# A two-layer graph kernel: fewer warm-up matmuls, list steps spread wider, paired tiles in the half chunk, and row stores later in the sync queue

## The chip, the cores and the metric

The kernel runs on one core of one Trainium2 chip. The metric is the device time of one execution in microseconds (us); lower is better. The five engines of the core have queues of their own: TensorE (PE, its weight loads shown as PEld), VectorE (DVE), ScalarE (ACT), GpSimd (POOL) and SyncE (SP), which here only issues transfers. Transfers are carried by the core's 16 DMA engines.

## The reference, cut to what matters

The data are 3327 nodes with 512 features and a weighted adjacency matrix of 3327 x 3327 that is dense in its first rows and columns ("hubs") and sparse elsewhere.

```python
# layer 0
h = jnp.maximum(_layernorm(x), 0.0)
u = jax.nn.relu(adj @ (h @ W1) + b1)          # W1: 512 x 128
x = x + adj @ (u @ W2) ... + b2               # computed as (adj @ u) @ W2 + b2
# layer 1
h = jnp.maximum(_layernorm(x), 0.0)
type_sum = adj @ h
attn_a, attn_b = sigmoid([type_sum, h] @ Wa.T + ba), sigmoid([type_sum, h] @ Wb.T + bb)
s_left, s_right = h @ W_sa @ a_sa[0, :512], h @ W_sa @ a_sa[0, 512:]
e = where(adj != 0, exp(-leaky_relu(s_left[:, None] + s_right[None, :], 0.01)), 0)
x_a = (e / (e.sum(1) + 1e-5)) @ (h @ W_sa)
x_b = adj @ (h @ W_gcnb) + b_gcnb
x = x + sigmoid(attn_a * x_a + attn_b * x_b)
```

The products with `adj` are the cost. Layer 0 has two of them, and the kernel makes each as a dense pass over the whole matrix. For layer 1 it gathers, for each group of 32 nodes, only the rows of h and the columns of adj in which something stands; which ones these are, it finds out during the first dense pass.

## The kernel before

The arrays are padded to 26 blocks of 128 rows (3328). The transposed matrix is read in column chunks: six of 512 columns and one of 256, the half chunk. There are three stages: the first dense pass (`acc_u`, 7 chunks of 26 blocks), the second dense pass (`acc_g`, 7 chunks), and the gather stage of layer 1.

The head warms TensorE up while the first rows of x are loaded and normalized:

```python
WAKE = 30
...
awake = bank(psB, "awake")
for _ in range(WAKE):
    nc.tensor.matmul(awake[:, :P], ident, ident, start=True, stop=True)
```

A tile of the matrix; both passes share eight buffers of 128 x 512 values, and all these loads are in the sync queue:

```python
def load_adj(j, c, name, n=1):
    c0, w = chunks[c]
    n = min(n, NB - j)
    t = adjp.tile([P, CW], F32, tag="adj", name=f"{name}_{c}_{j}")
    t = t[:, : n * w].rearrange("p (k i) -> p k i", i=w)
    rows = adjT[j * P : (j + n) * P, c0 : c0 + w]
    nc.sync.dma_start(t, rows.rearrange("(k p) i -> p k i", p=P))
    return t
```

The first pass. In its first chunk the rows are also normalized (`normalize`), transposed (`turn_h`, tile `pt`) and multiplied with W1 (`make_u`, tile `pu`). VectorE reduces every tile to the largest absolute value per group of 32 columns (`most`), from which the lists are made:

```python
for c in range(NCH):
    c0, w = chunks[c]
    acc = bank(psA, f"acc_u_{c}")
    most = l0w.tile([P, MG, NB], F32, tag="most", name=f"most_{c}")
    for j in range(NB):
        if c == 0:
            ...                       # load_x(j + 4), normalize(j + 3), turn_h(j + 2), make_u(j + 1)
        with queued(x_loaded[min(j + 4, NB - 1)] if c == 0 else None):
            a = load_adj(j, c, "a1")[:, 0, :]
        added = nc.tensor.matmul(acc[:, :w], u[j], a[:, :w], start=(j == 0), stop=(j == NB - 1))
        with queued(...):
            nc.vector.tensor_reduce(most[:, : w // GW, j], a[:, :w].rearrange(...), ...)
        if j >= 2:
            next(lists, None)         # one step of the lists of the chunk before
        if j % 3:
            gather_behind(added)      # GpSimd: one gather of columns, paced by this matmul
        ...
    chunk_end = make_g(c, acc)        # ScalarE: gT <- acc_u; PE: four transposes pg; VectorE: g
    with tc.issue_after(chunk_end.ins):
        if c == 1:
            load_weights()            # W2, b2 (then b2_row + 0.5 on VectorE), W_sa, ...
        ...
    lists = make_lists(c, most)
    next(lists)
```

The lists are made by a generator, a step at each `next`; what stands between two `yield` is put beside one block of the pass:

```python
def make_lists(c, most):
    ...                               # VectorE: flag, upto (a scan), count, after
    nc.vector.tensor_tensor(after[:, :n, :], ..., upto[:, :n, :], ALU.subtract)
    p_off = bank(psB, f"p_off_{c}")
    nc.tensor.matmul(p_off[:, :n], before, count[:, :n], start=True, stop=True)
    nc.tensor.matmul(p_off[:, MG : MG + n], every, count[:, :n], start=True, stop=True)
    ...                               # VectorE: offset, size
    nc.tensor.matmul(p_sh[:, : n * NB], shift, after[:, :n, :].rearrange(flat), ...)
    ...                               # VectorE: step
    yield
    ...
    for batch in batches:             # one to three batches for a chunk
        for i, q in batch:
            for h in range(2):
                nc.vector.tensor_scalar(at[:, k : k + r, h, :], place_row..., offset..., op0=ALU.is_ge)
            if (i, q) != batch[-1]:
                yield
        pl = bank(psB, f"p_list_{f0}")
        for i, q in batch:
            ...                       # PE: 2 * rooms[i] small matmuls p_list <- step, at
        yield
        ...                           # VectorE: past, jb, row_h, row_a
        listed.update(batch)
        yield
```

The second pass loads tiles for `per = CW // w` blocks, so the half chunk is paired there already. Beside each chunk stands the row work of the chunk before (`late`, one step at every second block):

```python
def make_h1(c, sT):
    c0, w = chunks[c]
    blocks = range(c0 // P, (c0 + w) // P)
    for b, i in enumerate(blocks):
        x1 = xs.pop(i)
        with tc.high_priority():
            ...                       # PE: px; VectorE: x1 = px + x1; ScalarE's queue: store of x1
            h = hrow[i % NR]
            _, last_row[0] = ln_relu(h[:, :D], x1, l0w, f"b{i}")
            score(i, h[:, :D], 1, h[:, D : D + 1])
            nc.sync.dma_start(h_dram[i * P : (i + 1) * P, :], h)
        if c:
            rows_made.add(i)
        yield
    for i in blocks:
        last_row[1] = score(i, hrow[i % NR][:, :D], 0, node[i][:, 0:1])
        yield
    ...                               # PE: four transposes pl <- node; ScalarE: s_left
    rows_made.update(blocks)
    yield
    for i in blocks:
        if c < NCH - 2:
            own_logits(i, ...)
        yield
```

`h_dram` is the table of h rows from which the gather stage later takes its rows. `acc_hub` matmuls for the first 128 nodes are mixed into the second pass from its third chunk on.

Of the kernel before, what the change touches and what calls it, by code (L numbers as in the profile page):

```python
# [26 lines left out]
SEG = 4  # L27
WAKE = 30
LN_EPS = 1e-5
# [17 lines left out]
def kernel(  # L47
# [35 lines left out]
    def bank(pool, name):  # L83
        return pool.tile([P, CW], F32, tag="bank", name=name)
# [94 lines left out]
    def queued(*insts):  # L179

        behind = ExitStack()
        for inst in insts:
            if inst is not None:
                behind.enter_context(tc.issue_after(inst.ins))
        return behind
# [30 lines left out]
    with (  # L216
# [167 lines left out]
        def make_lists(c, most):  # L384
# [5 lines left out]
            def small(shape, name, dtype, bufs=2):  # L390
# [16 lines left out]
                upto[:, :n, :], ALU.subtract,  # L407
            )
            p_off = bank(psB, f"p_off_{c}")
            nc.tensor.matmul(p_off[:, :n], before, count[:, :n], start=True, stop=True)  # L410
# [24 lines left out]
            for batch in batches:  # L435
# [7 lines left out]
                for i, q in batch:  # L443
                    r, k = rooms[i], col[i, q]
                    for h in range(2):
# [5 lines left out]
                        )  # L451
                    if (i, q) != batch[-1]:
                        yield
                pl = bank(psB, f"p_list_{f0}")
# [40 lines left out]
        for c in range(NCH):  # L495
            c0, w = chunks[c]
            acc = bank(psA, f"acc_u_{c}")
            most = l0w.tile([P, MG, NB], F32, tag="most", name=f"most_{c}")
            for j in range(NB):
                if c == 0:  # L500
# [6 lines left out]
                    if j + 1 < NB:  # L507
                        make_u(j + 1)
                with queued(x_loaded[min(j + 4, NB - 1)] if c == 0 else None):
                    a = load_adj(j, c, "a1")[:, 0, :]  # L510
                added = nc.tensor.matmul(  # L511
# [51 lines left out]
        def own_logits(i, junk):  # L563
# [6 lines left out]
            nc.vector.tensor_tensor(node[i][:, 1:3], node[i][:, 1:3], bab_row, ALU.add)  # L570

        def make_h1(c, sT):

            c0, w = chunks[c]
# [4 lines that stand above are left out]
# [8 lines left out]
                    score(i, h[:, :D], 1, h[:, D : D + 1])  # L587
                    nc.sync.dma_start(h_dram[i * P : (i + 1) * P, :], h)
                if c:
                    rows_made.add(i)  # L590
                yield
            for i in blocks:
                last_row[1] = score(i, hrow[i % NR][:, :D], 0, node[i][:, 0:1])
                yield
            pl = bank(psB, f"pl_{c}")
# [10 lines left out]
            if c == 0:  # L606
                nc.scalar.copy(s_hub, pl[:, :P])
            rows_made.update(blocks)
            yield
            for i in blocks:  # L610

                if c < NCH - 2:
                    own_logits(i, l0w.tile([P, D], BF16, tag="junk", name=f"junk_{i}", bufs=1))
                yield
# [482 lines left out]
```

## Time and profile before

| | |
|---|---|
| time, median of 3 runs | 781.73 us (780.81 to 782.48) |
| span of the profiled execution | 780.7 us, 12235 instructions |
| PE, PEld | 755.4 us (97%), 415.5 us (53%) |
| VectorE, ScalarE, GpSimd | 517.5 us (66%), 185.5 us (24%), 489.8 us (63%) |
| DMA | 200.15 MB, mean 256 GB/s |
| loads of 128 x 512 tiles, sync queue | 325 of 256 KB, median 4.0 us from issue to landing |
| loads of 128 x 256 tiles, sync queue | 26 of 128 KB, median 3.3 us |
| stores of h rows, sync queue | 26 of 260 KB, median 4.1 us |
| first dense pass, second dense pass | to 225.07 us, from there to 431.60 us |

In the profile one line is a group of instructions: line of the kernel, engine, operation, output and inputs, shape, count; a time in brackets is how long the engine stood idle before it and what ended that. A 128x512 matmul on 32-bit values stands as two records. The ends of matmuls are modelled, so where one waits for its data it may look busy; the distance between the starts of two records tells more. The issue of a transfer is not counted as busy.

### The profile page before, as it was taken

What the parts mean: (1) busy time and instruction counts of PE and PEld (TensorE: products, weight loads), DVE (VectorE), ACT (ScalarE), POOL (GpSimd) and SP (SyncE); (2) the same over time, 40 slices, a digit from 0 to 9 for tenths busy, and PEclk for the clock granted to TensorE, in tenths of its full rate; (3) what the DMA queues carried; (4) which work ended last, traced back from release to release, by engine and by line L of the source; (5) the groups of instructions that cost most, each with busy time, mean ns of one, the idle gap of its engine ahead of it and who ended that gap; (6) DMA issues with size and microseconds to landing.
All of it is one profiled execution on the core that took longest, in us unless ns stands there. A gap on an engine that the chain in (4) does not pass through costs nothing.

```text
span 780.7 us, 12235 instructions
## 1 busy us (share of the span) xinstructions
PE 755.4 (97%) x3647; PEld 415.5 (53%) x3647; DVE 517.5 (66%) x1658; ACT 185.5 (24%) x396; POOL 489.8 (63%) x513
## 2 busy tenths in 40 slices
PE   9999989999999999999999999999999999999995
PEld 8775434444544344344446456665665666655453
DVE  6768979999992876759577575555465464644542
ACT  6882000000000331403215212221221221311211
POOL 1400746666777777777773277677777777777720
PEclk9999999999999999999999999999999999999998
DMA  7888899889889999899998578688888888888840
GB/s 241 247 261 262 272 296 289 263 270 293 230 262 288 319 333 336 283 323 318 311 336 266 171 226 242 202 245 255 252 238 253 251 234 260 225 258 229 228 154 32
DMA packets 107099, 200.15 MB, mean 256 GB/s; under 512 B 17009, under 2 KB 30864, under 8 KB 107024
## 3 DMA queue, kind: packets, MB, share of 16 engines
q1 hardware_dynamic: 72800, 124.40, 48.7%
q0 software_dynamic: 25536, 63.74, 29.8%
q10 hardware_dynamic: 8688, 11.15, 4.3%
q8 instruction: 31, 0.51, 0.3%
q14 instruction: 44, 0.36, 0.2%
HBM read 179.39 MB, written 20.55 MB: 256 GB/s over the span
## 4 chain that ended last, share of the span: by engine, by line
PE 82%; DMA 7%; DVE 7%; issue 1%; ACT 1%; POOL 0%; SPq 0%; POOLq 0%; ACTq 0%; DVEq 0%
PE acc_u L511 16%; PE acc_g L665 14%; PE acc L809 13%; PE p_b L863 12%; PE p_a L870 11%; DMA a<-in_adjT_dram 6%; PE ptt L823 3%; PE pu L293 3%; PE acc_hub L624 2%; PE px L580 2%; PE p_list L459 2%; PE pt L285 1%; DVE junk L559 1%; DVE xb L583 1%; PE awake L100 1%
## 5 line engine op out<-in xcount | busy, mean ns | idle before, releaser
L139 POOL DMA_INDIRECT ae<-in_adjT_dram,row_a x228 | 244.2, 1071 | 145.2 <-DVE most L515 49.1
L139 POOL DMA_INDIRECT hr<-h_rows,row_h x140 | 143.5, 1025 | 47.0 <-issue 27.4
L511 PE MATMUL acc_u<-a,rows 128*128 128x512 f32 (+1 forms) x364 | 164.0, 580 | 1.5 <-DMA a<-in_adjT_dram 1.5
L665 PE MATMUL acc_g<-a,g 128*128 128x512 f32 (+1 forms) x364 | 156.4, 570 | 3.6 <-DMA a<-in_adjT_dram 3.4
L139 POOL DMA_INDIRECT rows<-h_rows,row_h x88 | 90.0, 1022 | 50.7 <-DVE e_hub L206 24.2
L515 DVE TENSOR_REDUCE most<-a 128x16 f32<-128x512 f32 (+1 forms) x182 | 111.1, 640 | 7.2 <-DMA a<-in_adjT_dram 6.8
L665 PEld LDWEIGHTS acc_g<-a,g 128*128 128x128 f32 x364 | 68.2, 192 | 80.1 <-issue 62.7
L863 PE MATMUL p_b<-W_g_sb,tyT 128*128 128x257 f32 x416 | 97.1, 386 | 0.8 <-ACT tyT L836 0.5
L870 PE MATMUL p_a<-W_sa_sb,tyT 128*128 128x512 f32 (+2 forms) x216 | 93.5, 577 | 0.0
L863 PEld LDWEIGHTS p_b<-W_g_sb,tyT 128*128 128x128 f32 x416 | 76.6, 189 | 30.8 <-DVE ae L206 7.3
L511 PEld LDWEIGHTS acc_u<-a,rows 128*128 128x128 f32 x364 | 63.9, 192 | 52.3 <-issue 45.8
L838 DVE COPY tyT<-ptt 128x512 f32<-128x512 f32 x51 | 34.9, 686 | 73.6 <-PE ptt L823 73.5
L809 PE MATMUL acc<-hr,ae 64*64 64x512 f32 x560 | 68.0, 607 | 0.0
L870 PEld LDWEIGHTS p_a<-W_sa_sb,tyT 128*128 128x128 f32 x216 | 41.0, 190 | 37.7 <-issue 35.9
L728 ACT ACTIVATE f<-f 128x2 f32<-128x2 f32 x26 | 5.3, 203 | 173.2 <-DVE f L727 145.8
L809 PE MATMUL acc<-rows,ae 64*64 64x512 f32 x352 | 42.5, 594 | 2.5 <-issue 1.8
L809 PEld LDWEIGHTS acc<-hr,ae 64*64 64x64 f32 x560 | 29.8, 136 | 23.4 <-issue 22.9
L302 ACT ACTIVATE gT<-acc_u,b_col 128x512 f32<-128x512 f32 (+1 forms) x7 | 4.6, 656 | 154.8 <-PE acc_u L511 97.9
L696 DVE TENSOR_TENSOR xb<-xb,b_row 128x512 f32<-128x512 f32 x26 | 17.7, 690 | 29.7 <-DMA xb<-in_x_dram 24.1
L559 DVE SCALAR_TENSOR_TENSOR junk<-rows,w_rows 128x512 bf16<-128x512 f32 x52 | 35.7, 687 | 1.9 <-ACT rows L201 0.9
L583 DVE TENSOR_TENSOR xb<-px,xb 128x512 f32<-128x512 f32 x26 | 16.9, 683 | 24.9 <-PE px L580 24.9
L823 PEld LDWEIGHTS ptt<-ident,ty 128*128 128x128 f32 x208 | 24.2, 141 | 14.2 <-issue 12.9
(142 smaller groups left out, 909.9 us busy)
## 6 DMA issues: line engine op xcount, KB each, us to landing
a<-in_adjT_dram SPq DMA_DIRECT2D x325, 256.0 KB, 4.0
h_rows<-rows SPq DMA_DIRECT2D x26, 260.0 KB, 4.1
x<-in_x_dram SPq DMA_DIRECT2D x26, 256.0 KB, 3.4
xb<-in_x_dram SPq DMA_DIRECT2D x26, 256.0 KB, 5.0
x<-xb ACTq DMA_DIRECT2D x26, 256.0 KB, 2.1
x1b<-x SPq DMA_DIRECT2D x26, 256.0 KB, 4.9
out_dram<-va SPq DMA_DIRECT2D x25, 256.0 KB
ae<-in_adjT_dram,row_a POOLq DMA_INDIRECT x228, 4.4
```

Source lines behind the costliest of these rows:

```text
L139: return nc.gpsimd.indirect_dma_start(out=dst, out_offset=None, in_=table, in_offset=bass.IndirectOffsetOnAxis(ap=rows, axis=0), bounds_ch ...
L293: nc.tensor.matmul(pu[:, :HID], hT[:, k, :], W1_sb[:, k, :], start=(k == 0), stop=(k == KD - 1))
L511: added = nc.tensor.matmul(acc[:, :w], u[j], a[:, :w], start=(j == 0), stop=(j == NB - 1))
L515: nc.vector.tensor_reduce(most[:, : w // GW, j], a[:, :w].rearrange("p (b i) -> p b i", i=GW), axis=AX.X, op=ALU.max, apply_absolute_value ...
L559: return nc.vector.scalar_tensor_tensor(junk, h, 1.0, w_rows[:, s, :], op0=ALU.mult, op1=ALU.mult, accum_out=into)
L583: nc.vector.tensor_tensor(x1, px, x1, ALU.add)
L665: added = nc.tensor.matmul(acc[:, :w], g[j], a[:, j % per, :], start=(j == 0), stop=(j == NB - 1))
L809: added = nc.tensor.matmul(taken[i]["acc"][h][q * HALF : (q + 1) * HALF, :], both[half_p, q * n + k, :], taken[i][k0][k][half_p, q, :D], s ...
L823: moved = nc.tensor.transpose(pt[:, k * P : (k + 1) * P], ty[h][:, k * P : (k + 1) * P], ident)
L838: last = nc.vector.tensor_copy(dst, src)
L863: nc.tensor.matmul(p_b[n][:, :WH], tyT[:, k, 0, :], W_g_sb[:, k, n * WH : (n + 1) * WH], start=(k == 0), stop=(k == KD - 1),)
L870: last = nc.tensor.matmul(p_a[:, c0:c1], tyT[:, k, 1, :], W_sa_sb[:, k, c0:c1], start=(k == 0), stop=(k == KD - 1),)
```

## The change

There are four edits; the first three concern the first pass, the last one the second.

- The head has 18 warm-up matmuls instead of 30.
- The list generator yields twice as often at its ends: once after `after`, before the p_off matmuls, and after every item of a batch, the last too. So the matmuls of a list step come a step later than the VectorE work that they read.
- In the half chunk of the first pass one load brings the tiles of two blocks, as in the second pass.
- The store of a row block in the h table is no longer issued where the row is made, but by a later step of the row work: block by block, from the third `score` step on. In the program that is ten to twelve blocks later. In the sync queue the four stood together behind the load of block 12 (of the next chunk); now they stand one by one behind the loads of blocks 13, 15, 17 and 19. The last two chunks' stores keep their places in the queue.

The aim is to have TensorE start earlier on real work, to keep it from waiting for VectorE's list work and for small tiles, and to keep tile loads from standing in the sync queue behind stores whose rows aren't made yet.

```diff
-WAKE = 30
+WAKE = 18
@@ make_lists
                 upto[:, :n, :], ALU.subtract,
             )
+            yield
             p_off = bank(psB, f"p_off_{c}")
@@ make_lists, batches
-                    if (i, q) != batch[-1]:
-                        yield
+                    yield
                 pl = bank(psB, f"p_list_{f0}")
@@ first pass
             acc = bank(psA, f"acc_u_{c}")
+            per = CW // w
@@
-                with queued(x_loaded[min(j + 4, NB - 1)] if c == 0 else None):
-                    a = load_adj(j, c, "a1")[:, 0, :]
+                if j % per == 0:
+                    with queued(x_loaded[min(j + 4, NB - 1)] if c == 0 else None):
+                        tile_a = load_adj(j, c, "a1", per)
+                a = tile_a[:, j % per, :]
@@ make_h1
+        def store_row(i):
+            nc.sync.dma_start(h_dram[i * P : (i + 1) * P, :], hrow[i % NR])
+
@@
-                    nc.sync.dma_start(h_dram[i * P : (i + 1) * P, :], h)
+                    if c == NCH - 1:
+                        store_row(i)
                 if c:
                     rows_made.add(i)
                 yield
-            for i in blocks:
+
+            unstored = iter(blocks if c < NCH - 1 else ())
+
+            def store_next():
+                for i in unstored:
+                    store_row(i)
+                    break
+
+            for b, i in enumerate(blocks):
                 last_row[1] = score(i, hrow[i % NR][:, :D], 0, node[i][:, 0:1])
+                if b > 1:
+                    store_next()
                 yield
@@
             rows_made.update(blocks)
+            store_next()
             yield
             for i in blocks:
+                store_next()
```

## The prediction

> **What bounds the kernel now.** The page says TensorE 97% busy, which hides the question: the ends of matmuls are modelled, so a matmul that waits for its tile can count as busy. I therefore cut the span into stages. The ends of the seven column chunks of the first pass are the starts of the copies out of acc_u (67.56, 94.04, 126.57, 154.55, 180.33, 206.15, 225.07 us), those of the second pass the copies out of acc_g (250.62 to 431.60 us). The stage table (columns: stretch, length, busy time of PE, PEld, DVE, ACT, POOL, granted clock, DMA share, GB/s):
>
> ```profile
> 94.04:126.57 32.53, 28.95 (x148) 12.88 (x147) 26.81 (x70) 0.69 (x1) 17.92 (x18) 0.95 0.91 293
> 154.55:180.33 25.78, 25.78 (x124) 11.40 (x123) 24.67 (x64) 0.69 (x2) 17.06 (x17) 1.00 0.91 281
> 206.15:225.07 18.92, 17.39 (x108) 10.48 (x107) 17.58 (x65) 0.69 (x2) 14.29 (x14) 1.00 0.75 206
> 250.62:281.08 30.46, 28.97 (x65) 12.38 (x64) 22.36 (x75) 7.99 (x17) 23.93 (x22) 0.94 0.97 318
> 281.08:313.52 32.44, 31.87 (x77) 13.84 (x76) 22.24 (x76) 8.90 (x17) 25.28 (x23) 1.00 1.01 339
> 313.52:347.24 33.72, 31.70 (x77) 13.92 (x76) 22.33 (x76) 8.91 (x18) 26.76 (x23) 1.00 0.92 306
> ```
>
> In the undisturbed timeline the records of a 128x512 matmul start 0.43 us apart; two make one block, so a chunk of 26 blocks costs PE 26 x 0.86 = 22.4 us. The fifth chunk (second row) comes near it: 22.4 plus 64 small list matmuls. But VectorE is busy 24.67 of its 25.78 us. The first pass is thus bound by PE with VectorE just beside it; the third chunk (first row) is 6.7 us longer. In the second pass a full chunk from the third on is 22.4 + 3.4 (eight px records) + 5.2 (twelve acc_hub records) + 0.4 = 31.4 us of PE, so the row of 32.44 us is nearly PE alone, at 339 GB/s. Next I read who ended PE's waits, then the places themselves:
>
> ```profile
> PE acc_g L665 <- DMA a<-in_adjT_dram: 3.4, 4, 2.0
> PE p_list L459 <- DVE at L447: 2.8, 2, 2.5
> ...
> PE pl L597 <- DVE junk L559: 1.7, 5, 0.4
> PE acc_u L511 <- DMA a<-in_adjT_dram: 1.5, 5, 0.4
> ```
> ```profile
> 96.64 0.35 PE L421 MATMUL p_sh<-after,shift 128*128 128x416 bf16 x1 [0.88 <-DVE after L405]
> ...
> 103.10 1.42 PE L459 MATMUL p_list<-step,at 128*64 128x27 bf16 x35 [2.54 <-DVE at L447]
> 104.44 2.92 PE L511 MATMUL acc_u<-a,rows 128*128 128x512 f32 x3
> ```
> ```profile
> DVE past L465 <- PE p_list L459: 3.8, 6, 1.4
> DVE most L515 <- DMA a<-in_adjT_dram: 3.4, 7, 1.2
> DVE b_row L257 <- DMA b_row<-in_b_dram: 2.9, 1, 2.9
> ```
> ```profile
> 324.88 3.07 SPq L588 DMA_DIRECT2D h_rows<-rows  x4
> 328.05 10.49 SPq L229 DMA_DIRECT2D a<-in_adjT_dram  x13
> ```
> ```profile
> 332.76 1.55 PE L665 MATMUL acc_g<-a,g 128*128 128x512 f32 x3 [2.02 <-DMA a<-in_adjT_dram]
> ```
> ```profile
> 1.43 8.59 PE L100 MATMUL awake<-ident 128*128 128x128 f32 x60 [1.43 <-POOL ident masks.py:199]
> 6.22 1.50 ACT L201 ACTIVATE h<-x,ln_a 128x512 f32<-128x512 f32 x2
> 9.86 1.04 PE L285 MATMUL pt<-ident,h 128*128 128x128 f32 x8
> ```
>
> The reader sees: PE waits for the list work in the third chunk and then runs three records in 2.92 us, at half rate; the VectorE lines are its waits over the second to sixth chunks, 10.5 us in all, which is all the air it has there; in the second pass the sync queue stands at four stores, then sends eight loads in a burst that lands too late; and in the head PE is busy with warm-up matmuls until 10.0 us though two tiles of h were ready at 7.7.
>
> **What the Trainium skill says.** (1) "TensorE: Matmul & The Clock Gate", Part 1: the array starts at half rate and is released after some 3.4 us of work, by time and not by count. The trace agrees: the warm-up records start 213 ns apart until 4.8 us, 3.4 us after the first, then 111 ns. (2) The same part says idling brings half rate back. The trace agrees after the 2.5 us wait at 103 us, though shorter than a window of idling that the page names. (3) "PSUM — Partial Sum Buffer", Engine vs sequencer instructions: the queues of VectorE and ScalarE are strictly first in, first out, and matmuls start in program order. The trace agrees: the b_row addition waits and nothing of VectorE passes it. (4) "DMA: Bandwidth & Descriptors", Anatomy of one DMA: a semaphore wait is served at the issuing sequencer before dispatch, so a store that waits for its data holds back the loads behind it; the rows at 324.88 and 328.05 are that. Its Specifications give about 358 GB/s for one core from HBM; the best stage here has 339.
>
> **The change part by part.**
>
> *Warm-up 30 to 18.* 12 matmuls are 24 records; at 111 ns that is 2.7 us, all in the fast part. The first pt then starts at about 7.2 instead of 9.86, when the first h is ready (6.97). The first copy of pt moves from 10.50 to about 7.9, when ScalarE has made its second h and a square root: 2.6 us. From there to 67 us PE has no wait in the timeline at a pitch of 2.19 us per block, DMA at 0.83 share and 269 GB/s, so the shift should hold. Gain 2.6.
>
> *List steps.* Nothing is added or removed but the order. In the changed order the p_off and p_sh matmuls stand two blocks later, and each group of p_list matmuls one to three blocks later and unbroken. Visible in the third chunk: 1.03 between p_off and p_sh, 2.74 in front of p_list, 1.4 of half rate, some 0.5 in small gaps; 0.6 in the second chunk, 0.9 in the fourth: 7.1 us. But the addition of b_row still stands ahead of the scale comparisons (`at`) in VectorE's queue and still waits for its transfer; only two blocks, 1.7 us, are put beside it. And VectorE has 128.1 us of work in those five chunks (138.6 us), so PE can't gain more than VectorE's waits shrink: of 10.5, the 2.9 for b_row stay, the 3.8 for p_list mostly go, the 3.4 for tiles partly. I take 4.5.
>
> *Half chunk.* 26 loads of 128 KB become 13 of 256 KB, in the same 8 buffers. PE's need is 52 records of 0.216 = 11.2, plus some 2.5 of list matmuls: 13.7, against 18.92. Eight small tiles are 8 x 0.43 = 3.4 us of PE, less than the 3.3 to landing and the issue; eight pairs are 6.9. VectorE then decides: 17.58 busy, of which 3 x 0.68 + 0.2 us (the `junk_w` sums) move into the next chunk, where VectorE has 12.5 busy of 25.6. Left are 15.3, so I take 3.5 and not 5.
>
> *Stores ten tiles later.* Each store now stands alone between loads, the first after the load of block 13. The loads no longer wait for VectorE's row work. In the third to sixth chunks of the second pass the starts of PE's records show 0.74, 2.18, 0.77 and 0.30 us lost there, 4.0. I take 3.0. In the second chunk of that pass the four pl transposes stand at 265 us for VectorE's row sums (each 0.63 beyond its 0.11, 2.7 with the edges), then 1.4 of half rate; the changed order has them five blocks later, 4.3 us, after the sums are done, and the tile loads that came as a burst at 262.74 are not held. That is 4.1, but the chunk carries 30.46 x 318 = 9.7 MB: in 26.4 us it would need 367 GB/s, above the 339 seen. I take 2.5.
>
> Sum: 2.6 + 4.5 + 3.5 + 3.0 + 2.5 = 16.1. The gather stage, from 431.6 us to the end, isn't touched: 349 us shift as they are. For waits that the new orders bring I take off about 15%, 2.4. 781.7 - 13.7 = 768.0 us.
>
> **The rivals.** *VectorE is the bound of the first pass.* Then the list order is worth only VectorE's shorter waits, and work moved into the first chunk of the second pass makes the pw transposes wait. For it: 24.67 of 25.78 busy, and the reductions release the tile buffers. Against: its 10.5 us of waits really stand beside the list matmuls. It would leave 2 us for the list steps and 2 for the half chunk: 772.
>
> *DMA fills the place of the stores.* The second pass moves 51.5 MB in its five middle chunks (160.7 us, 320 GB/s). If 325 is what it can hold beside gathers, only 2.3 us come off instead of 5.5, and PE's waits for the stores turn into waits for late tiles: 771. For it: shares of 0.97 and 1.01. Against: 339 was held for a whole chunk.
>
> *Everything adds.* If the half-rate stretches vanish with the idling and DMA gives 339, 7.1 + 5 + 4 + 4 + 2.6 = 22.7 us come off: 759. *The head is not PE's.* If the tile x_5, loaded only when the first h is done (7.04 us), lands too late, the head gives 1 us.
>
> **Range and chances.** The parts don't depend on each other much, each uncertain by 1 to 2 us, together about 4 us around 768.0, with a longer tail to little gain, since PE, VectorE and DMA all lie within 5% of each other: 763.0 to 774.5. Two per cent is 15.6 us, 766.1; some third lies below it. Nothing lengthens by 2%: no work is added and the stores end before the gathers need them. Faster by over 2%: 0.33; within: 0.66; slower: 0.01.
>
> **What would show each step.** Right: first pt at about 7.2 us and the first chunk's end near 65; the third chunk at 28 to 30 us with p_list waits under 1.5; the half chunk at 15 to 16 us without PE waiting for tiles; the chunks of the second pass at 31.5 to 32.5, no row of four stores in the sync queue and under 1 us of PE's waits for tiles there; pl without waits. Wrong: VectorE's waits gone but chunks no shorter; GB/s in the second pass stuck at 320 with PE waiting for tiles; pw waiting over 1 us after the half chunk; a later stage longer than 349 us.

## The result and the profile after

The changed kernel takes 761.95 us (median of 6 runs, 760.76 to 766.43), the kernel before on the same chip 782.71 us (780.81 to 785.13): a ratio of 0.9741, 95% interval 0.9712 to 0.977. So 20.8 us came off, where the prediction had 13.7; the time lies 1 us below the range. The profiled spans are 758.9 and 780.7 us.

Cut at the same copies out of acc_u and acc_g as in the prediction, the stages changed so (us):

| stage | before | after | difference |
|---|---|---|---|
| first chunk of the first pass | 67.56 | 65.69 | -1.9 |
| second to sixth chunk | 26.48, 32.53, 27.97, 25.78, 25.82 | 26.06, 29.83, 25.96, 24.88, 24.82 | -7.0 |
| half chunk | 18.91 | 15.02 | -3.9 |
| first chunk of the second pass | 25.55 | 24.96 | -0.6 |
| second chunk of it | 30.46 | 26.73 | -3.7 |
| third to sixth | 32.44, 33.71, 32.29, 31.83 | 32.85, 31.42, 31.42, 31.42 | -3.2 |
| its half chunk and the gather stage | 369.3 | 367.8 | -1.5 |

The stage table of the changed kernel, for the same six stages that the prediction shows of before, in the same order and with the same columns (stretch, length, busy time of PE, PEld, DVE, ACT, POOL, granted clock, DMA share, GB/s):

```profile
91.76:121.59 29.83, 27.93 (x148) 12.69 (x147) 27.26 (x71) 0.69 (x2) 18.33 (x18) 0.94 0.99 320
147.55:172.44 24.89, 24.89 (x124) 11.32 (x123) 24.86 (x64) 0.69 (x2) 17.09 (x17) 1.00 0.92 297
197.25:212.28 15.03, 14.88 (x108) 11.14 (x107) 14.21 (x56) 0.69 (x2) 11.47 (x12) 1.00 0.83 238
237.23:263.96 26.73, 26.64 (x64) 11.14 (x62) 21.43 (x74) 7.79 (x17) 21.25 (x19) 1.00 1.00 345
263.96:296.81 32.85, 31.64 (x77) 14.37 (x78) 23.35 (x78) 8.79 (x17) 25.85 (x24) 1.00 1.01 344
296.81:328.24 31.43, 31.43 (x77) 13.98 (x76) 22.34 (x76) 8.91 (x18) 24.72 (x23) 1.00 0.97 325
```

Two rows tell most. In the second, the fifth chunk, PE and VectorE are both busy from end to end (24.89 and 24.86 of 24.89 us). Since the ends of matmuls are modelled, the starts have to say whether PE works or waits there, and they do below. In the last, PE is busy for all of 31.43 us, the sum of its matmuls that the prediction had worked out (31.4); nothing but PE's own work is left there. The fourth row is a chunk at 345 GB/s, above what the prediction took for the most.

PE's line of work in the fifth chunk, first a piece of the kernel before, then of the changed one:

```profile
160.96 1.13 PE L511 MATMUL acc_u<-a,rows 128*128 128x512 f32 x2
162.01 0.30 PE L459 MATMUL p_list<-step,at 128*64 128x27 bf16 x8
162.25 3.70 PE L511 MATMUL acc_u<-a,rows 128*128 128x512 f32 x8
```
```profile
155.20 0.68 PE L459 MATMUL p_list<-step,at 128*64 128x27 bf16 x32
155.81 5.42 PE L514 MATMUL acc_u<-a,rows 128*128 128x512 f32 x12
161.16 0.68 PE L459 MATMUL p_list<-step,at 128*64 128x27 bf16 x32
```

In the kernel before five groups of small list matmuls stand between the big ones, in the changed kernel two. From 160.96 to 162.25 us are 1.29 us; two big records take 0.86 of them, and eight small ones take 0.12 where they stand inside a large group (two every 0.031 us). So about 0.3 us go at the two ends of each group, an estimate from these spacings, and three groups fewer are worth the 0.9 us by which the chunk got shorter. Within both kernels' fifth chunks no two starts of PE lie more than 0.58 us apart: PE works there all the time and waits for nothing, before as after. In the fourth to sixth chunks together the groups went from 19 to 8 and the length from 79.6 to 75.7 us, with 0.2 us of waits of PE before and none after. In the second chunk there are 3 groups instead of 4, in the third 3 instead of 6.

PE's waits in the changed kernel, the two longest from the end of the first chunk to the end of the second pass; after the colon stand us in all, times, and the longest:

```profile
PE p_list L459 <- DVE at L448: 2.2, 3, 1.8
PE acc_g L684 <- DMA a<-in_adjT_dram: 1.2, 1, 1.2
```

VectorE's waits over the second to sixth chunks of the first pass, same columns:

```profile
DVE b_row L257 <- DMA b_row<-in_b_dram: 2.4, 1, 2.4
DVE most L518 <- DMA a<-in_adjT_dram: 1.3, 2, 1.1
DVE past L465 <- PE p_list L459: 0.3, 2, 0.2
```

VectorE's wait for the p_list matmuls is all but gone (3.8 before), its waits for tiles fell from 3.4 to 1.3, and that for b_row is nearly what it was. In sum 10.5 became 4.0.

The timeline of PE in the third chunk (start, length, count, and in brackets the wait ahead of it):

```profile
100.35 1.51 PE L459 MATMUL p_list<-step,at 128*64 128x27 bf16 x36 [1.82 <-DVE at L448]
101.79 5.40 PE L514 MATMUL acc_u<-a,rows 128*128 128x512 f32 x8
```

So the wait at this place didn't go: it is 1.82 us instead of 2.54, and the eight records behind it still take 5.40 us where eight at 0.43 are 3.4. Half rate came back after that wait as it did before: the granted clock is 0.50 from 102.15 to 105.56 us.

The sync queue in the fourth chunk of the second pass (start of the issue, length, count):

```profile
307.87 0.38 SPq L576 DMA_DIRECT2D h_rows<-rows  x1
308.35 0.91 SPq L229 DMA_DIRECT2D a<-in_adjT_dram  x2
309.35 0.42 SPq L576 DMA_DIRECT2D h_rows<-rows  x1
```

The four stores no longer stand in a row of 3.07 us; each takes 0.4 us and the tile loads go on between them.

The head:

```profile
1.43 6.72 PE L100 MATMUL awake<-ident 128*128 128x128 f32 x36 [1.43 <-POOL ident masks.py:199]
7.99 1.04 PE L285 MATMUL pt<-ident,h 128*128 128x128 f32 x8
```

The first transposes start at 7.99 us, 1.87 earlier, not at 7.2. That is this one profile: over the profiles of the first twelve experiments below and these two they start at 7.20 to 8.47 us with 18 warm-up matmuls and at 9.86 to 10.94 with 30.

Last, the matmuls of one block near the end of the gather stage, the one with the longest list: first in the kernel before, then in the changed one.

```profile
730.93 1.09 PE L809 MATMUL acc<-rows,ae 64*64 64x512 f32 x8 [1.80 <-issue]
731.82 7.91 PE L809 MATMUL acc<-hr,ae 64*64 64x512 f32 x56
```
```profile
710.42 1.09 PE L828 MATMUL acc<-rows,ae 64*64 64x512 f32 x8 [1.24 <-issue]
711.30 6.22 PE L828 MATMUL acc<-hr,ae 64*64 64x512 f32 x56
```

The same 64 records, after a wait that is 0.56 us shorter, took 1.7 us less: the longer wait was followed by half rate, the shorter was not. This is nearly all of the 1.5 us that the last row of the table gains. The stage isn't touched by the change, and from this block's predecessors back, over 262 us, the two profiles agree within 0.01 us. The end part, counted from the weight matmuls (p_b) that stand ahead of this block, took 59.8 us before and 58.0 after, and 56.6 to 59.3 in the profiles of the first twelve experiments below, whatever their edits. I put the 1.5 us down to the chance of one profile.

### The profile page after: what moved, and what is told of

Read it like the earlier page. It is cut to its first block, busy times and chain, and to the rows that moved or that the text cites. A ratio compares the mean times of both kernels' runs of the same rounds, so it can differ in the third digit from the quotient of the medians.

```text
span 758.9 us, 12159 instructions
## 1 busy us (share of the span) xinstructions
PE 740.5 (98%) x3623; PEld 411.8 (54%) x3623; DVE 516.9 (68%) x1658; ACT 185.2 (24%) x396; POOL 490.8 (65%) x513
## 5 line engine op out<-in xcount | busy, mean ns | idle before, releaser
L514 PE MATMUL acc_u<-a,rows 128*128 128x512 f32 (+1 forms) x364 | 158.5, 573 | 0.0
L684 PE MATMUL acc_g<-a,g 128*128 128x512 f32 (+1 forms) x364 | 154.7, 564 | 1.3 <-DMA a<-in_adjT_dram 1.2
L828 PE MATMUL acc<-hr,ae 64*64 64x512 f32 x560 | 66.2, 593 | 0.0
```

What stands on the lines that cost most here:

```text
L684: added = nc.tensor.matmul(acc[:, :w], g[j], a[:, j % per, :], start=(j == 0), stop=(j == NB - 1))
L828: added = nc.tensor.matmul(taken[i]["acc"][h][q * HALF : (q + 1) * HALF, :], both[half_p, q * n + k, :], taken[i][k0][k][half_p, q, :D], s ...
```

## The experiments

The theory that the experiments were made to try: in the second to sixth chunks of the first pass the length is VectorE's work plus VectorE's waits, and the list steps took away more of these waits than the prediction had allowed; nothing was lost to new waits; and the stores cost their place in the sync queue and not DMA's capacity. The rivals: the gain lies in one of the other edits and shows up in those chunks (an earlier head, fewer loads); or DMA fills the place of what is removed.

A ratio is that to the kernel before, run on the same chip in the same rounds; "stage" values come from one profile each, and such values scatter: the second to sixth chunks took 131.0 to 135.8 us in eight kernels whose first pass differs at most in the head and the half chunk. The table near the end therefore also has means over profiles.

### One part alone

Four kernels, each the kernel before with one of the four edits.

```diff
 e1_head:    WAKE = 18
 e2_lists:   + yield ahead of p_off;  yield after every item of a batch
 e3_pairs:   tile_a = load_adj(j, c, "a1", per) at every per-th block of the first pass
 e4_stores:  store_row / store_next in make_h1
```

> Only the warm-up is shortened (18 instead of 30). Theory A, the parts add up as the stage lengths of the two profiles show them: the first chunk ends about 1.9 us earlier (65.7 instead of 67.6) and everything behind it shifts, so 780.9 where the kernel before has 782.7. Theory B, VectorE bounds the first pass and takes the gain back in the second to sixth chunks: the first chunk ends earlier all the same, but the first pass ends less than 1 us earlier and the time is within 0.7 us of before.

> Only the list steps are spread. Theory A: the second to sixth chunks lose 0.4, 2.7, 2.0, 0.9 and 1.0 us as between the two profiles, 7.0 in all; VectorE's waits for p_list there fall from 3.8 to under 0.5 us and those for tiles from 3.4 to some 1.3; 775.7. Theory B, the prediction's own size: VectorE's waits only partly go, 4.5 us, 778.2. Theory C, part of those 7 us came from the other edits (the earlier head, the order around them): under 4 us.

> Only the half chunk's tiles are paired. Theory A: the half chunk is 15.0 us instead of 18.9, PE waits for no tile in it, and the first chunk of the second pass is not longer than 25.6 though it takes over the w_col sums: 4 to 4.5 us off, 778.4. Theory B, VectorE bounds it: the half chunk stays over 16.5 us, 2 us off. The list order is the old one here, with list matmuls that break the chunk up in small groups, so A may show 0.5 us less than in the changed kernel.

> Only the row stores come later. Theory A: the pl transposes move five blocks back and the loads flow, the second chunk of the second pass is 26.7 instead of 30.5 us and the third to sixth together lose 3.2: 6.9 us off, 775.8; GB/s in that second chunk near 345. Theory B, the prediction's: DMA holds no more than 339 GB/s, so 5.5 us off. Theory C, DMA fills the place: under 3 us off and PE waits for late tiles.

| | before on this chip | time | ratio, interval | the stage it is meant for |
|---|---|---|---|---|
| e1_head | 785.19 | 785.77 | 1.0006, 0.9984 to 1.0028 | first chunk 67.56 -> 65.18 |
| e2_lists | | 775.53 | 0.9869, 0.9801 to 0.9936 | second to sixth chunk 138.6 -> 132.2 |
| e3_pairs | | 782.40 | 0.9959, 0.9941 to 0.9977 | half chunk 18.91 -> 16.07 |
| e4_stores | | 776.34 | 0.9887, 0.9813 to 0.9962 | second pass 206.5 -> 200.5 |

The head's edit does what it is meant to in its own stage (2.4 us), and nothing of it is left in the time. In its profile the third chunk is 1.5 us longer than before (34.01), the fourth 0.5, and the second pass 2.9 (209.4), where PE waits 7.3 us for tiles instead of 3.4. But e3_pairs, with the old head, waits 7.0 us there and has a second pass of 209.6, so this profile doesn't show where the 2.4 us went; that stays open. The lists have the largest effect, 6.4 us by stages and 9.7 by times, in the chunks where they stand. The four gains by time, -0.6, 9.7, 2.8 and 8.9, sum to 20.8, about the whole change; their intervals of 1.4 to 6 us each way make that sum rough.

### The whole change less one part

```diff
 f1_all:       the changed kernel again
-f2_no_head:   WAKE = 18
+f2_no_head:   WAKE = 30
-f3_no_lists:  the two new yields
-f4_no_pairs:  tile_a = load_adj(j, c, "a1", per)
+f4_no_pairs:  a = load_adj(j, c, "a1")[:, 0, :]
```

> The changed kernel again, as the ground for the three that each take one edit back. Both theories: 20.8 us under the kernel before, the third to sixth chunks of the second pass at 31.4 us each.

> The changed kernel with 30 warm-up matmuls again. Alone, the shorter warm-up made the first chunk 2.4 us shorter and the time no shorter. Theory A: what it gained was lost in the second pass, where the stores made PE's waits a matter of chance; with the stores out of the way it reaches the end, so this kernel is 1.9 to 2.4 us slower than the whole change. Theory B: it is lost in the third chunk, where VectorE waits for b_row, whose transfer doesn't come sooner; then the third chunk is shorter here by some 1.5 us and the time within 0.7 us of the whole change.

> The changed kernel with the old list steps. Theory A, list order alone worth what the stages say: the second to sixth chunks take 7 us more, time 7 us more. Theory B, the prediction's size: 4.5 us more. Theory C, the half chunk needs the list order too (alone the pairs made it 16.1 and not 15.0 us): 8 us more, with the half chunk at 16 us.

> The changed kernel with single tiles in the half chunk. Alone the pairs took 2.8 us off that chunk in the profile and 3.2 us off the time. Theory A: with the list order they are worth more, half chunk 18.0 as with the lists alone, plus a longer first chunk of the second pass (26.4 instead of 25.0): 4.4 us slower than the whole change. Theory B, worth what they were alone: 3 us slower.

| | time | ratio (before: 785.83), interval | worse than f1_all by | by its stage |
|---|---|---|---|---|
| f1_all | 763.19 | 0.9721, 0.9664 to 0.9778 | | |
| f2_no_head | 766.81 | 0.9763, 0.9709 to 0.9817 | 3.6 | first chunk 1.7 |
| f3_no_lists | 771.87 | 0.9811, 0.9758 to 0.9864 | 8.7 | second to sixth chunk 8.8 (139.9 for 131.0) |
| f4_no_pairs | 767.29 | 0.976, 0.9702 to 0.9817 | 4.1 | half chunk 4.7 (19.78 for 15.10) |

The intervals of f2_no_head and f4_no_pairs overlap that of f1_all for the most part, so their 3.6 and 4.1 us are not shown by the time alone; the runs of f3_no_lists (770.5 to 772.8 us) all lie above those of f1_all (761.5 to 766.7). The half chunk needs the list order for its last microsecond: with the pairs but without the yields it is 15.79 us in f3_no_lists and 16.07 in e3_pairs.

Without its two yields the kernel has every other edit, and VectorE's waits over the second to sixth chunks are those of before again. In f3_no_lists:

```profile
DVE most L518 <- DMA a<-in_adjT_dram: 4.7, 8, 1.3
DVE past L465 <- PE p_list L459: 3.4, 5, 1.5
DVE b_row L257 <- DMA b_row<-in_b_dram: 3.0, 1, 3.0
DVE step L424 <- PE p_sh L421: 0.5, 1, 0.5
```

These sum to 11.6. Take the sum from the length of the five chunks, in four kernels:

| | length | VectorE's waits | rest |
|---|---|---|---|
| before | 138.6 | 10.5 | 128.1 |
| f3_no_lists | 139.9 | 11.6 | 128.3 |
| e2_lists | 132.2 | 4.9 | 127.3 |
| after | 131.6 | 4.0 | 127.6 |

The rest, VectorE's work, is the same within 1 us in these four, and 125.1 to 128.4 us over the thirteen profiles of the two kernels and of all experiments down to e8_act_store. That is bookkeeping, though, for an engine either works or waits, and it doesn't say which engine sets the pace. In the fourth to sixth chunks VectorE's waits (2.6 us before, 0.4 after) went while PE, for which it mostly waited, worked without a gap: there the gain is PE's, from the ends of groups that it no longer has, and VectorE's waits follow. These three chunks take 79.3 to 80.3 us in the five profiles without the yields and 75.7 to 78.2 in the eight with them. In the third chunk PE does wait for VectorE.

The rival that another edit shortens these chunks is out: with all others and without the yields they are no shorter than before. VectorE's waits for p_list are 2.5 to 5.1 us in the five profiles without the yields and 0.2 to 1.5 in the eight with them. Its waits for tiles fall too in these four kernels (4.7 and 3.4 without the yields, 1.3 and 2.2 with them), but reach 6.4 us in e8_act_store, which has the yields; that they go with the list waits isn't shown.

In the half chunk the profile of f4_no_pairs has this row (columns of the stage table):

```profile
198.60:218.39 19.79, 16.71 (x108) 10.12 (x106) 16.71 (x62) 0.69 (x2) 15.22 (x16) 1.00 0.70 196
```

PE and VectorE are both idle for 3 us, at 196 GB/s against 238 with pairs: tiles come too late there, though DMA has room.

### Stores back, stores elsewhere, loads apart, b_row early

```diff
 e6_no_stores, against the changed kernel
-                    if c == NCH - 1:
-                        store_row(i)          # and all store_next()
+                    nc.sync.dma_start(h_dram[i * P : (i + 1) * P, :], h)
 e7_two_loads, against the changed kernel: one buffer, filled by two loads
-                tile_a = load_adj(j, c, "a1", per)
+                for k in range(n):
+                    nc.sync.dma_start(t[:, k, :], adjT[(j + k) * P : (j + k + 1) * P, c0 : c0 + w])
 e8_act_store, against e6_no_stores: the same place, ScalarE's queue
-                    nc.sync.dma_start(h_dram[i * P : (i + 1) * P, :], h)
+                    nc.scalar.dma_start(h_dram[i * P : (i + 1) * P, :], h)
 e9_b2_early, against the changed kernel: the load of b2_row a chunk earlier
+                if c == 0:
+                    nc.scalar.dma_start(b2_row, b2.partition_broadcast(P))
```

> The changed kernel with the stores where they were. The fourth of the kernels that take one edit back. Theory A: with four stores in a row the second pass is again a matter of late bursts: its second chunk 28.5 to 30.5 us, the third to sixth 131 to 135 us together instead of 127, so 7 to 11 us slower than the whole change (ratio to before 0.981 to 0.987). Theory B, the prediction's size of 5.5 us: ratio 0.979.

> The changed kernel with the pair of tiles of the half chunk still in one buffer, but brought by two loads of 128 KB. Theory A, it is the depth in bytes (eight buffers of 256 KB instead of 128) that took PE's waits away: half chunk 15 to 15.5 us, ratio as the whole change. Theory B, it is the number of loads in the queue (each issue some 0.4 us, 26 of them in 11 us): half chunk over 17 us, ratio 0.977.

> The changed kernel, but each row store is issued as soon as its row is made, in ScalarE's queue and not in the sync queue; no store stands ahead of a tile load. Theory A, it is the place in the sync queue that costs: the second pass is as in the changed kernel (second chunk about 27, third to sixth about 127.5 us), though the four stores still follow each other at once; time within 2 us of the whole change, ratio 0.972 to 0.975. Theory B, it is the bunching of the store traffic that hurts, and the change helps by spreading it: third to sixth chunks over 130 us, ratio 0.979 or more.

> The changed kernel with the transfer of b_row issued one chunk earlier, so that it lies in SBUF when VectorE comes to its addition. Theory A, the third chunk's remaining excess (29.8 against 24.9 us for the fifth) is VectorE's wait of 2.4 us for that transfer and the half rate after it: third chunk 26 to 27 us, 3 us faster than the whole change, ratio 0.970. Theory B, the third chunk is bound by its transfers (weights and hub columns, 320 GB/s): 28.5 us or more, under 1 us faster.

| | time | ratio (before: 783.22), interval | stage |
|---|---|---|---|
| e6_no_stores | 771.87 | 0.9838, 0.9786 to 0.989 | second pass 205.5, PE's waits for tiles in it 4.5 |
| e7_two_loads | 763.78 | 0.9736, 0.9691 to 0.9781 | half chunk 15.40; second pass 199.9 |
| e8_act_store | 762.36 | 0.9704, 0.9654 to 0.9754 | PE's waits for tiles in the second pass 1.1 |
| e9_b2_early | 766.60 | 0.9762, 0.9693 to 0.983 | second chunk 31.01, third 28.37 |

With the stores back in their places the kernel loses 8.1 us to e7_two_loads beside it, and the queue looks like that of before. The sync queue in the fifth chunk of the second pass of e6_no_stores:

```profile
343.66 3.07 SPq L591 DMA_DIRECT2D h_rows<-rows  x4
346.82 4.20 SPq L229 DMA_DIRECT2D a<-in_adjT_dram  x8
```

The eight loads go out right behind the stores, one every 0.5 us where PE takes one in 0.86, so several of their buffers had been free already and the stores had held the loads up. PE then waits 1.88 us for a tile that comes at 351.69 us. In e8_act_store the rows are stored about as early, but by ScalarE's queue. Three of the four stores in its fourth chunk:

```profile
311.02 6.31 ACTq L591 DMA_DIRECT2D h_rows<-rows  x3
```

PE's waits for tiles fall to 1.1 us, as little as with late stores (0.6 to 3.1 in eight profiles, 3.4 to 7.3 in five with the stores in their old places). So the early stores cost nothing once they don't stand ahead of tile loads. Their expected bunching did not happen, however: the four are issued over 7.2 us here, from 309.82 us on, and within 2.75 us in e6_no_stores, so a cost of four stores close together isn't excluded. The rival by which DMA fills the place falls: the bytes are the same in all of these.

The two loads into one buffer keep the half chunk short:

```profile
197.34:212.74 15.40, 15.01 (x107) 10.89 (x105) 14.57 (x57) 0.69 (x1) 11.78 (x12) 1.00 0.79 221
```

It is 15.40, against 14.96 to 15.11 with one load in kernels with the new list steps and 19.78 with a buffer for each half tile. Most of the gain of the pairs is thus the depth in bytes (eight buffers that hold 256 KB instead of 128 KB each), and not the halved number of loads.

e9_b2_early took the b_row wait away from the third chunk, which became 1.5 us shorter (28.37), and moved the trouble one chunk ahead. The stage row of its second chunk, 26.06 us long in the changed kernel:

```profile
65.08:96.09 31.01, 29.29 (x156) 13.36 (x155) 25.16 (x61) 0.69 (x1) 12.15 (x12) 0.89 0.75 225
```

PE waits 1.7 us there for p_list in three pieces, then runs at half rate (clock 0.50 from 75 to 80 us), and DMA moves 100 GB/s in those five microseconds. VectorE waits 4.7 us for tiles in the chunk, most of it before that stretch (2.47 us up to 70.47 us). Why the tiles came late just there stays open. The load of one small row, moved by a chunk, cost 5 us in one place and gained 1.5 in another, in this one profile.

### The two yields apart, and the third chunk

On the two chips of these last six runs every kernel, the one before too, took some 851 us where it had taken 783, with engines standing where the trace shows no releaser; what follows the sixth chunk of the second pass took 419.8 to 429.4 us instead of 366.8 to 371.0. Only their ratios, their own waits and the lengths of the chunks beside each other are used.

```diff
 g0_first_yield, against before:   + yield ahead of p_off, only
 g1_second_yield, h1_second_yield, against before:   yield after every item, only
 g2_b2_late, against the changed kernel: the addition to b_row moved from the second chunk's end to the fourth's
+                if c == 3:
+                    nc.vector.tensor_scalar(b2_row, b2_row, 0.5, None, op0=ALU.add)
 g3_spread, h2_spread: g2, and the other weights later
+                if c == 2:
+                    nc.scalar.dma_start(W_sa_sb, W_sa.rearrange("(k p) f -> p k f", p=P))
+                if c == 4:
+                    nc.scalar.dma_start(w_own, ...); nc.scalar.dma_start(bab_row, ...)
```

> The kernel before with the first of the two new yields alone: the p_off and p_sh matmuls stand two blocks later, the p_list groups stay broken up. Theory A: the greater part of the list gain is p_list's (VectorE's 3.8 us behind p_list and the small pieces between PE's blocks), so the second to sixth chunks lose 2 us of the 6.4 that both yields together took off them. Theory B: PE's and VectorE's waits around p_off and p_sh set the later ones off, and this yield alone brings 4 us or more.

> The kernel before with the second new yield alone: p_list groups later and unbroken, p_off and p_sh where they were. Theory A: 4 to 5 us off the second to sixth chunks, with VectorE's wait for p_list under 1 us and the 0.9 us of PE before p_sh still there. Theory B: under 2.5 us.

> The changed kernel with VectorE's addition of b_row two chunks later, its transfer where it was, so VectorE doesn't wait for it and no transfer moves. Theory A: the third chunk's excess is VectorE's wait and the half rate behind it: that chunk 26 to 27.5 us instead of 29.8, no wait of PE for p_list in it, and 2.5 us off the time, ratio 0.970. Theory B: the weights and hub columns that are loaded in that chunk make it bound by DMA (share 0.99, 320 GB/s): it stays over 28.5 us and PE waits for tiles instead.

> As the one before, and the 1.0 MB of W_sa is loaded one chunk later and the 0.5 MB of w_own three chunks later. Theory A: nothing beyond the kernel before it in this row, as the third chunk isn't bound by DMA. Theory B: another 1 to 2 us off the third chunk, and the fourth and sixth not longer.

| | time | ratio (before: 850.72), interval | second to sixth chunk |
|---|---|---|---|
| g0_first_yield | 851.89 | 1.0011, 0.9974 to 1.0048 | 30.33, 32.30, 28.16, 25.79, 25.49 |
| g1_second_yield | 853.18 | 1.0035, 1.0011 to 1.0059 | 25.98, 31.46, 28.12, 26.31, 27.01 |
| g2_b2_late | 839.52 | 0.9858, 0.9795 to 0.992 | 26.62, 29.60, 27.06, 26.21, 26.31 |
| g3_spread | 837.51 | 0.9826, 0.9762 to 0.9889 | 25.81, 29.07, 27.92, 26.22, 26.30 |

Two of them again, on the second such chip:

> The second new yield alone once more, on whatever chip comes, as the first time fell on a chip on which every kernel took some 65 us more. Theory A: 4 to 5 us off the second to sixth chunks of the first pass (138.6 us before), VectorE's wait for p_list under 1 us; ratio to before 0.993 to 0.995. Theory B: under 2.5 us, the first yield is needed too; ratio over 0.997.

> The whole change with the b_row addition two chunks later and W_sa and w_own loaded in later chunks, once more. Theory A, the third chunk's excess in the changed kernel (29.8 us against 24.9) is b_row's wait: 26 to 27 us, and 3 us off the time, ratio to before 0.969. Theory B, that chunk is bound by DMA or by the head of its list work: over 28 us, ratio as the whole change, 0.973.

h1_second_yield took 851.59 us beside 851.87 (0.9996, 0.9969 to 1.0024), h2_spread 840.75 (0.9863, 0.9832 to 0.9894).

No gain of either yield alone could be measured on these chips; g1_second_yield even took 2.5 us more. Three of the kernels here have both yields (g2_b2_late, g3_spread and h2_spread, with b_row's addition later), and their five chunks sum to 135.8, 135.3 and 134.6 us, against 142.1 with the first yield alone and 138.9 and 139.1 with the second alone. With the second alone PE waits 3.7 and 3.9 us ahead of p_off in these chunks (2.2 us of the latter for VectorE's `count`); with both it doesn't wait there. So the two yields seem to need each other on these chips; on the others neither was tried alone. The four edits with b_row's addition moved brought 11.1 to 13.2 us there, where the changed kernel had 20.8 elsewhere. The third chunk with everything moved away, in h2_spread:

```profile
91.35:120.00 28.65, 27.18 (x148) 12.40 (x147) 28.05 (x72) 0.68 (x1) 18.47 (x19) 1.00 0.92 295
```

VectorE has no wait for b_row any more and is busy for 28.05 of 28.65 us, where in the changed kernel it was for 27.26 of 29.83. So this chunk too is nearly VectorE's work now, of which it simply has more than the fifth (24.86). But g2_b2_late has no such wait either, and its third chunk is 29.60 us, with PE waiting 1.0 us for tiles at a DMA share of 1.01. The third chunk stays over 28.5 us in all three kernels, as the second theories of g2_b2_late and h2_spread had it. How much the b_row wait by itself is worth in the third chunk isn't settled. None of these versions was shown to beat the changed kernel; e8_act_store (0.9704) can't be told from it.

## Why the prediction was off, point by point

| term of the sum | predicted | by stages, after | by stages, means | alone, by time | taken out, by time |
|---|---|---|---|---|---|
| head | 2.6 | 1.9 | 2.4 | -0.6 | 3.6 |
| list steps | 4.5 | 7.0 | 6.2 | 9.7 | 8.7 |
| half chunk | 3.5 | 3.9 and 0.6 in the chunk behind | 3.6 and 0.3 | 2.8 | 4.1 |
| stores, third to sixth chunk | 3.0 | 3.2 | 5.3 | 8.9 with the next row | 8.1 with the next row |
| stores, second chunk | 2.5 | 3.7 | 2.2 | | |
| new waits | -2.4 | 0 | | | |
| gather stage | 0 | 1.5 | | | |

The means are over the thirteen profiles of the two kernels and of all experiments down to e8_act_store: each stage with the edit meant for it against the same stage without it (e8_act_store is left out of the stores). They sum to 20.0 us.

**The mechanisms named did act, and the sum failed by size**, in the list steps, the discount and the stores; in the list steps a cost was left out of the working.

*List steps, the step that failed.* "PE can't gain more than VectorE's waits shrink: of 10.5, the 2.9 for b_row stay, the 3.8 for p_list mostly go, the 3.4 for tiles partly. I take 4.5." The chunks gave 7.0, and 6.2 on the mean. PE's losses had been counted where PE was seen to wait or to run at half rate, and for the fourth to sixth chunks that made 0.9 us. They gave 3.9, though PE had next to no waits there: what went was 11 groups of small matmuls with some 0.3 us at the ends of each, a cost of the old order that shows as work and that the count did not have. The count's 7.1 agrees with the 7.0 only in sum, for the third chunk, for which 5.7 of it stood, gave 2.7. "P_list waits under 1.5" was wrong; one of 1.82 us stayed, with its half rate. As a limit VectorE's waits held: they shrank by 6.5 (p_list by 3.5, tiles by 2.1, b_row by 0.5, step by 0.4), but taken as the cause they hid what PE itself would gain.

*New waits.* "For waits that the new orders bring I take off about 15%, 2.4." None came. The chunk behind the half chunk, where the pw wait was feared, got shorter (24.96 for 25.55). A discount that no line of the profile asked for was a third of the miss.

*Stores.* "In 26.4 us it would need 367 GB/s, above the 339 seen. I take 2.5." The chunk ran in 26.73 us at 345 GB/s and gave 3.7. Two things were wrong: the highest rate seen so far was taken as the highest possible, and the bytes as fixed. At 345 GB/s for 26.73 us the chunk moved 9.2 MB and not 9.7, since a shorter stretch also holds fewer of the gathers that run beside it (19 instead of 22). But part of the 3.7 is chance: the 30.46 us before hold a stretch of half rate (clock 0.94), and two of the five profiles with the old stores have none and take 28.48 and 28.67 us. On the mean the chunk gave 2.2. The other four chunks gave 3.2 for 3.0, the third of the pass nothing, and the fourth to sixth fell to PE's bare 31.42. Here the profile before was a mild one, with 3.4 us of PE's waits for tiles where the four others with the old stores have 4.5 to 7.3, and the mean gain is 5.3. The term was thus read off one profile that showed too little: 5.5 in all, against 6.9 in the two profiles, 7.5 on the mean and 8 to 9 by the times.

*Half chunk.* 15.02 us lies where it was put (15 to 16). "VectorE then decides" was wrong: VectorE is busy for 14.21 of 15.03 us, while PE's big records start 0.22 us apart all through, with some 0.3 us more at each of six groups of list matmuls. The reason was right in kind, time to fetch against depth of buffer; e7_two_loads shows that it is the bytes and not the count of loads.

*Head.* "At 111 ns that is 2.7 us, all in the fast part." In the changed kernel's profile the fast part began later: 23 records of the warm-up started 213 ns apart (5.1 us with a longer first one), where the kernel before had 15 (3.4 us). So 1.9 in place of 2.6. This differs from profile to profile, and on the mean the first chunk gave 2.4, so the term itself was right. That the shift holds through the later stages was assumed; alone, it didn't.

*Gather stage.* The 1.5 us is the block with the long list, most likely chance.

In sum, 2.5 us of list steps, 2.4 of discount, 1.4 of stores, 1.0 of the half chunk with the chunk behind it and 1.5 of chance, less 0.7 of the head, are 8.1; the spans differ by 21.8 and not 13.7, which is that. By the means it is 1.7 of list steps, 2.4 of discount, 2.0 of stores and 0.4 of the half chunk with the chunk behind it, less 0.2 of the head: 6.3 of the 7.1 us by which the time was missed.

**The rivals.** "VectorE is the bound of the first pass" was wrong in its 772, for it left 2 us to the lists, and in the fourth to sixth chunks and the half chunk PE's starts speak against it; the prediction's own "bound by PE with VectorE just beside it" fits them. "DMA fills the place of the stores" is false. "Everything adds", 759, was nearest, though not for its reason, since the half-rate stretch stayed and the head gave less. The chances were too timid: the parts were independent enough that a sum of shown losses should not have been cut.

## What to carry to other kernels

Where an engine shows as busy all the time, look at the distances between the starts of its instructions: they tell its work from its waits, and here they also showed what many small groups between big matmuls cost, which no wait showed. An engine's waits and its work always sum to the stage; ask of each wait which engine it follows from before taking it as the thing to gain. Read a stage off several profiles, for one profile missed a stage by 2 us here. Don't put a store that waits for an engine ahead of the loads of a prefetch in one queue; a later place or another queue did equally well here. The highest rate that a profile shows is what was needed, not what the chip can give.

## What the runs showed of the hardware

- A group of small matmuls between big ones cost PE about 0.3 us at its ends, without any wait: in the fifth chunk two 128x512 records and a group of eight took 1.29 us, the two alone take 0.86 and eight more inside a large group 0.12.
- Half rate came back after shorter waits than I had expected: after one of 1.82 us in the third chunk and one of 1.80 us in the gather stage, but not after 1.24 us there. And the slow start of the same warm-up matmuls lasted 15 records in the profile before and 23 in the one after, 3.4 and 5.1 us; over all twenty profiles it lasted 14 to 28 records, 3.1 to 6.1 us. The Trainium skill, "TensorE: Matmul & The Clock Gate", Part 1, puts both states down to a window of some 3.4 us that runs freely and isn't started by the kernel, so that the length of the warm-up varies from run to run. The trace agrees with the varying warm-up, and the half-rate stretch in the third chunk is 3.41 us long; that a wait of half a window, with small matmuls beside it, brings half rate back is less than the page names.
- A chunk of 26.73 us moved 345 GB/s, and one slice of 19 us on the changed kernel's page 366, reads and writes together. The prediction quoted some 358 for a core. The Trainium skill, "Perfetto Trace Analysis", Roofline, calls that the share of a core when both of a pair are active, and says that a core alone can pull more; the 366 agrees.
- Two chips differed from the others by some 9% for the same kernel (851 against 783 to 786 us).
